# Other VectorE durations in the build-time planner of a two-layer graph kernel

## The chip, the cores and the metric

The kernel runs on one core of one Trainium2 chip. The metric is the device time of one launch in microseconds (us), and the median of the runs of the kernel before is 1470.73 us.

## What is computed

There are 16 graphs of 1024 nodes with 64 channels each, and a dense 1024x1024 adjacency per graph that is mostly zero. The mask is all ones in the given inputs.

```python
h = max(layernorm(x), 0)
x = x + matmul(adj / clip(adj.sum(2), 1), h)                       # layer 0
h = max(layernorm(x), 0)                                           # layer 1
nb = neighbours of each node in adj, without itself; m = their number
rows with m > 10 drop every ceil(m/2)-th neighbour, and the drop is made symmetric
agg = 0.25*q25 + 0.5*q50 + 0.25*q75 over the node itself and the neighbours left
x = x + (relu((h + agg) @ W1 + b1) @ W2 + b2) * mask
```

The quantiles are taken per node and per channel over a list whose length differs from node to node.

## The kernel before, in words

**Layer 0 (eight streams, lines 574 to 823).** Each graph is taken in eight blocks of 128 adjacency rows. `loads` brings a block in (SP queue), `signs` makes a 16-bit sign copy of it on ScalarE, `listing` (line 631) multiplies that by a key on VectorE (`sg<-sg,keyed`) and takes the eight largest of four segments with MAX8 (`rec<-sg`), which lists the neighbours. `transposes` and `products` make the matmul on TensorE, with evacuations on ScalarE; `channels` makes the layernorm of layer 1; `endings` (line 751) sorts the nodes of a graph by list length in a chain of small VectorE operations and scatters their rows with eight indirect DMAs per graph from the POOL queue (`srt<-row,to`).

**Layer 1 (class `Job`, line 845).** The graphs form four groups of four. `group` (line 1187) prepares a group's tables once its four graphs are through. A job then takes the nodes whose lists have one length. It gathers the neighbours' rows, one indirect DMA per 128 rows and place (`places<-tab,idx`, POOL queue), masks and weighs them on VectorE, sorts them in `passes` (line 982) with a min/max network of `tensor_tensor` operations, weighs the sorted places, and sends the sums through TensorE and ScalarE (`layers`, line 1124) to an indirect scatter into the output (`out_dram<-y`). Four long jobs at the end (`long_lists`, line 1324; tiles `lplaces`, `lother`, `l0other`) serve the few nodes with 16 to 88 neighbours. A network operation is 64 channels wide times the number of 128-row tiles in the job times the pairs that it takes at once, so most of them are 64 to 512 elements wide in each partition.

**What sets the order.** VectorE's and POOL's instructions are kept in the order in which the Python program issues them (`tc.manual_schedule`), and the program issues them in the order of a planner, which is no part of what runs on the chip. Every piece of work is a generator, a stream, that yields an engine and a function that tells from when it could run. `Plan.run` (line 335) takes, again and again, the stream with the smallest pair of planned start and rank: a start is the larger of the engine's planned clock and the time that the stream names. `Plan.note` (line 283) moves the clock of the engine forward by the planned duration of each instruction, and says that its output can be read `after` later. POOL's indirect DMAs are planned at 1.27 us, with 2.2 us to landing. Streams ask for margins: `SLACK` 2 us after an operand from another engine, `LOOSE` 7 us, `LATE` 14 us (lines 227 to 229). Jobs rank ahead of layer 0 while fewer than `AHEAD` = 16 gathers are outstanding and behind it otherwise (`later` and `soon`, lines 913 to 919). Buffers count too: there are four `places`, four `sg`, five `at`, six `y` tiles.

`passes` does not let `note` look at tiles. It keeps its own table of places and says (line 996) that a network operation's result can be used 0.15 us after VectorE's planned clock:

```python
soon = max(done.get(key, begin) for key in near)
yield "DVE", lambda: soon, self.later
...
done.update(((copy, i + shift), plan.clock["DVE"] + 0.15) for i in each)
```

`spread` (line 201) is called by `network` (line 155) once per network, ahead of the planner. It puts the operations of one network into the order in which the planner gets them: the one whose operands are ready first, the first of the list among equals.

All instructions of the planned part have line L240 in the profile, the line of the wrapper, so groups are told apart by their tiles. A slow path for graphs that don't fit the lists (`dense_path`) is behind a branch that isn't taken.

Of the kernel before, what the change touches and what calls it, by code (L numbers as in the profile page):

```python
# [125 lines left out]
def numbers(run):  # L126
    first, d1, n1, d2, n2 = run
    return [first + d2 * k2 + d1 * k1 for k2 in range(n2) for k1 in range(n1)]
# [26 lines left out]
def network(n, width, block=None):  # L155
# [16 lines left out]
    for layer in reversed(layers):  # L172
# [17 lines left out]
        for (part, _, is_max, *kind), left in sorted(kinds.items()):  # L190
# [3 lines left out]
            )  # L194
    parts = [
        spread([op for p, op in ops if p == part], width) for part in range(1 + -(-n // block))
    ]
    return parts, count, at


def spread(ops, width):

    left, order = list(ops), []
    clock, ready = 0.0, {}
    while left:
        best, reads, writes = None, set(), set()
        for k, (op, ai, aj, dist, copy, run) in enumerate(left):
            run = numbers(run)
            near = {(ai, i) for i in run} | {(aj, i + dist) for i in run}
            out = {(copy, i + (dist if op == OP.max else 0)) for i in run}  # L210
            if not (near & writes or out & (reads | writes)):
                begin = max(clock, *(ready.get(key, 0.0) for key in near))
                if best is None or begin < best[0]:
                    best = begin, k, out
            reads |= near
            writes |= out
        begin, k, out = best
        clock = begin + 0.07 + len(numbers(left[k][5])) * width * 1.04e-3
        ready.update((key, clock + 0.15) for key in out)
        order.append(left.pop(k))  # L220
    return order
# [24 lines left out]
class Plan:  # L246
# [36 lines left out]
    def note(self, engine, op, args, kwargs):  # L283
        if self.own is not None:
            self.clock[engine] = max(self.clock[engine], self.own)
        out = kwargs["out"] if "out" in kwargs else args[0]
        rest = [*args[0 if "out" in kwargs else 1:], *(v for k, v in kwargs.items() if k != "out")]
        rest = [getattr(v, "ap", v) if type(v).__name__.startswith("Indirect") else v for v in rest]
        rest = [v for v in rest if isinstance(v, bass.AP)]
        size = max(math.prod(v.shape[1:]) for v in (out, *rest[:2]))  # L290
        start = max(
            self.clock[engine],
            *(self.ready.get(v.tensor.name, 0.0) for v in rest if self.own is None),
            self.used.get(out.tensor.name, 0.0) if self.own is None else 0.0,
        )
        after = 0.15
        apart = engine == "SP" and out.tensor.name in self.parts
        if apart:
            start = max(self.clock[engine], *(self.ready[v.tensor.name] for v in rest))
        if engine == "DVE":  # L300
            half = op == "tensor_tensor" and all(v.dtype == HF for v in (out, *rest))
            time = 0.04 if op == "memset" else 0.07 + size * (0.57e-3 if half else 1.04e-3)
        elif engine == "ACT":
            pointers = sum(isinstance(kwargs.get(k), bass.AP) for k in ("bias", "scale"))
            time = 0.06 + size * 0.86e-3 + 0.11 * pointers + 0.09 * ("accum_out" in kwargs)
        elif engine == "PE":
            time = 0.1 + math.prod(out.shape[1:]) * 0.88e-3
            if op == "matmul" and rest[0].dtype == F32:
                time *= 2
        elif engine == "POOL":  # L310
            time, after = (1.27, 2.2) if op == "indirect_dma_start" else (0.15, 0.1)
            self.last = None
        else:
            start = max(start, self.clock["DMA"])
            busy = math.prod(out.shape) * 4 / 165e3

            time, after = 0.05, 2.2 + busy * (1 if 4 * out.shape[-1] >= 512 else 2)
            self.clock["DMA"] = start + busy
        self.clock[engine] = end = start + time
        if not apart:  # L320
            self.ready[out.tensor.name] = end + after
        for v in rest:
            self.used[v.tensor.name] = max(self.used.get(v.tensor.name, 0.0), end + after)
        if "accum_out" in kwargs:
            self.ready[kwargs["accum_out"].tensor.name] = end + after
        return start
# [1438 lines left out]
```

## Time and profile before

| what | value |
|---|---|
| median of 3 runs | 1470.73 us (1468.12 to 1472.69) |
| the profiled execution's own time | 1469.38 us |
| its span | 1467.6 us |
| VectorE (DVE) | 1267.8 us busy, 86%, 4263 instructions |
| GpSimd (POOL) | 939.3 us busy, 64%, 1112 instructions |
| TensorE matmul (PE) | 738.8 us busy, 50% |
| ScalarE (ACT) | 577.8 us busy, 39% |
| indirect gathers of `places` and `lplaces` | 621, from 213.94 us on, the last one ends at 1379.5 us |

A record gives an instruction's start and end. Where records of one engine lie over each other, the busy time counts the stretch once. POOL's busy time holds the records of its indirect DMAs, and a DMA that is issued right behind another starts 0.30 us after the end of that one's record, so 1.25 us pass from start to start of two gathers in a row.

### The profile page before, as it was taken

What the parts mean: (1) busy time and instruction counts of PE and PEld (TensorE: products, weight loads), DVE (VectorE), ACT (ScalarE), POOL (GpSimd) and SP (SyncE); (2) the same over time, 40 slices, a digit from 0 to 9 for tenths busy, and PEclk for the clock granted to TensorE, in tenths of its full rate; (3) what the DMA queues carried; (4) which work ended last, traced back from release to release, by engine and by line L of the source; (5) the groups of instructions that cost most, each with busy time, mean ns of one, the idle gap of its engine ahead of it and who ended that gap; (6) DMA issues with size and microseconds to landing.
All of it is one profiled execution on the core that took longest, in us unless ns stands there. A gap on an engine that the chain in (4) does not pass through costs nothing.

```text
span 1467.6 us, 14957 instructions
## 1 busy us (share of the span) xinstructions
PE 738.8 (50%) x3186; PEld 460.6 (31%) x3186; DVE 1267.8 (86%) x4263; ACT 577.8 (39%) x1747; POOL 939.3 (64%) x1112
## 2 busy tenths in 40 slices
PE   4778777228778347683585663200510101224864
PEld 2444334214445224352353332100410001123753
DVE  6878799999999895899959967588999998999895
ACT  7989879245666324783454432000100000000110
POOL 0132227777767777577876777477777787778432
PEclk9889898559989558895598676555665555555876
DMA  5446667424464224465233232321211111221000
GB/s 175 150 145 185 163 192 196 119 67 112 135 164 141 66 51 112 129 194 136 69 93 96 82 71 48 63 68 41 43 39 24 25 30 31 44 46 24 16 11 11
DMA packets 134591, 132.22 MB, mean 90 GB/s; under 512 B 100196, under 2 KB 102884, under 8 KB 134372
## 3 DMA queue, kind: packets, MB, share of 16 engines
q1 hardware_dynamic: 102972, 91.00, 21.6%
q0 software_dynamic: 31520, 40.19, 12.6%
q14 instruction: 72, 0.59, 0.1%
q8 instruction: 27, 0.44, 0.1%
HBM read 111.62 MB, written 23.61 MB: 92 GB/s over the span
## 4 chain that ended last, share of the span: by engine, by line
DVE 44%; POOL 19%; issue 11%; ACT 10%; DMA 9%; PE 5%; SPq 1%; DVEq 0%; POOLq 0%; ACTq 0%
POOL places L240 11%; DVE places L240 7%; DVE other L240 6%; DVE lplaces L240 5%; DVE rec L240 5%; DMA at<-in_adj_dram 4%; DMA places<-tab,idx 4%; POOL lplaces L240 4%; ACT sg L240 3%; PE pt L240 3%; ACT ln_sq L240 2%; DVE l0other L240 2%; DVE sg L240 2%; POOL out_dram L240 2%; PE ps_small L240 2%
## 5 line engine op out<-in xcount | busy, mean ns | idle before, releaser
L240 POOL DMA_INDIRECT places<-tab,idx x372 | 371.6, 999 | 115.5 <-issue 105.7
L240 PE MATMUL pt<-ident,prod 128*128 128x128 f32 (+1 forms) x736 | 162.5, 384 | 396.4 <-DVE prod L240 320.3
L240 PEld LDWEIGHTS pt<-ident,prod 128*128 128x128 f32 (+1 forms) x736 | 132.9, 264 | 428.1 <-issue 255.7
L240 PE MATMUL ps_small<-att,h 128*65 128x512 f32 x512 | 255.0, 645 | 14.1 <-ACT att L240 6.7
L240 POOL DMA_INDIRECT srt<-row,to x128 | 128.1, 1001 | 178.5 <-ACT row L240 156.0
L240 PE MATMUL pt<-ident,at 128*128 128x128 f32 x1024 | 167.1, 308 | 93.9 <-ACT att L240 71.7
L240 DVE MAX8 rec<-sg 128x8 f16<-128x256 f16 x512 | 180.2, 414 | 4.4
L240 PEld LDWEIGHTS pt<-ident,at 128*128 128x128 f32 x1024 | 128.0, 156 | 139.0 <-ACT att L240 95.3
L240 ACT ACTIVATE sg<-at 128x1024 f16<-128x1024 f32 x128 | 135.0, 1055 | 89.9 <-DMA at<-in_adj_dram 69.6
L240 POOL DMA_INDIRECT lplaces<-whole,lidx x125 | 132.1, 1057 | 38.3 <-issue 37.4
L240 POOL DMA_INDIRECT places<-tab,last_idx x124 | 126.2, 1018 | 37.8 <-issue 36.3
L240 ACT COPY att<-pt 128x512 f32<-128x512 f32 x256 | 141.4, 583 | 19.0 <-PE pt L240 17.6
L240 PEld LDWEIGHTS ps_small<-att,h 128*65 128x65 f32 x512 | 74.0, 151 | 148.2 <-issue 119.7
L240 ACT COPY ot<-pt 128x128 f32<-128x128 f32 (+3 forms) x56 | 22.4, 399 | 230.2 <-PE pt L240 228.1
L240 DVE TENSOR_TENSOR sg<-sg,keyed 128x1024 f16<-128x1024 f16 x128 | 87.3, 682 | 29.4 <-ACT sg L240 29.3
L240 POOL DMA_INDIRECT out_dram<-y,nodes_i x93 | 97.0, 1043 | 21.0 <-issue 13.9
L240 ACT ACTIVATE wu<-wu 128x39 f32<-128x39 f32 (+9 forms) x40 | 9.5, 237 | 255.2 <-DVE wu L240 255.2
L240 PE MATMUL ps_small<-ot,w_sb 128*128 128x128 f32 (+3 forms) x112 | 49.4, 531 | 100.4 <-DVE y L240 84.1
L240 ACT ACTIVATE hid<-ps_small,b_sb 128x128 f32<-128x128 f32 (+2 forms) x56 | 28.1, 504 | 126.3 <-PE ps_small L240 126.0
L240 DVE TENSOR_TENSOR other<-places,other 128x64 f32<-128x64 f32 (+6 forms) x204 | 69.4, 340 | 5.4
L240 DVE TENSOR_TENSOR places<-places,other 128x64 f32<-128x64 f32 (+2 forms) x208 | 62.3, 309 | 4.8
L240 DVE TENSOR_TENSOR places<-other,places 128x128 f32<-128x128 f32 (+5 forms) x160 | 54.9, 343 | 3.4
(269 smaller groups left out, 1651.3 us busy)
## 6 DMA issues: line engine op xcount, KB each, us to landing
at<-in_adj_dram SPq DMA_DIRECT2D x128, 512.0 KB
places<-tab,idx POOLq DMA_INDIRECT x372
whole<-tab SPq DMA_DIRECT2D x4, 1057.0 KB
tab<-row SPq DMA_DIRECT2D x16, 264.0 KB
xt<-in_x_dram SPq DMA_DIRECT2D x16, 256.0 KB
srt<-row,to POOLq DMA_INDIRECT x128
lplaces<-whole,lidx POOLq DMA_INDIRECT x125
places<-tab,last_idx POOLq DMA_INDIRECT x124
```

Of the source, the lines that this page charges most:

```text
L240: ins = getattr(self._engine, op)(*args, **kwargs)
```

## The change

Six numbers in the planner. In `spread` the fixed part of a network operation goes from 0.07 to 0.15 us. In `note` the fixed part of a VectorE operation goes from 0.07 to 0.12 us (0.10 where all operands are 16-bit in a `tensor_tensor`), that of a `memset` from 0.04 to 0.06 us, and the time until its output can be read from 0.15 to 0.05 us. The factors per element stay. The 0.15 in `spread`'s `ready` and in `passes` (line 996), and the 0.07 with which `passes` decides where to put a small `memset` (line 999), stay too. No instruction is added or taken away; VectorE's and POOL's can come in another order.

```diff
@@ spread @@
-        clock = begin + 0.07 + len(numbers(left[k][5])) * width * 1.04e-3
+        clock = begin + 0.15 + len(numbers(left[k][5])) * width * 1.04e-3
         ready.update((key, clock + 0.15) for key in out)
@@ Plan.note @@
         if engine == "DVE":
+            after = 0.05
             half = op == "tensor_tensor" and all(v.dtype == HF for v in (out, *rest))
-            time = 0.04 if op == "memset" else 0.07 + size * (0.57e-3 if half else 1.04e-3)
+            time = 0.06 if op == "memset" else (
+                0.1 + size * 0.57e-3 if half else 0.12 + size * 1.04e-3
+            )
```

## Prediction

> **What bounds the kernel now.** I read the page's slices first, then the waits of the two queues that the planner orders, then the timeline of VectorE for what one instruction costs its queue.
>
> ```profile
> DVE  6878799999999895899959967588999998999895
> POOL 0132227777767777577876777477777787778432
> ...
> DVE 44%; POOL 19%; issue 11%; ACT 10%; DMA 9%; PE 5%; SPq 1%; DVEq 0%; POOLq 0%; ACTq 0%
> ```
>
> In 40 slices of 36.7 us VectorE is at 9 tenths from the sixth slice on, with holes in slices 16, 21 and 24 to 26. POOL stands mostly at 7, and that is full: a gather's record is 0.94 us, and 0.30 us of issue lie between two (the longest line below: 466 such gaps, 142.0 us). From 213.94 to 1379.5 us the timeline shows 837 indirect DMAs on POOL and 12 waits above 0.5 us, 57.8 us in all. VectorE in the same stretch has 19 waits above 1 us, 82.3 us in all. The chain ends on both. The kernel is a two-queue pipeline with 5 to 7% of air, and the order of the queues decides where the air is.
>
> ```profile
> POOL places L240 <- issue: 142.0, 466, 0.3
> POOL lplaces L240 <- issue: 37.4, 122, 0.6
> POOL srt L240 <- ACT row L240: 25.0, 14, 10.2
> ...
> POOL gat_rows L240 <- DVE gfound L240: 14.8, 1, 14.8
> ```
>
> ```profile
> DVE sg L240 <- ACT sg L240: 22.1, 3, 8.7
> DVE rem L240 <- DMA places<-tab,idx: 11.4, 5, 3.6
> DVE gat_rows L240 <- DMA gat_rows<-in_adj_dram,lnodes_i: 10.9, 3, 5.6
> DVE y L240 <- PE ps_small L240: 10.8, 2, 6.0
> DVE deg L240 <- PE ps_small L240: 9.2, 1, 9.2
> ```
>
> Both are the waits between 213 and 1380 us (engine, tile, what ended the wait, us in total, times, longest). After 1214 us VectorE has only 4.8 us of such waits up to 1380 us: the end is a VectorE backlog, so what VectorE loses before it is mostly lost for good.
>
> **What an instruction costs VectorE's queue.** The timeline of one network, 64 elements wide:
>
> ```profile
> 496.76 0.23 DVE L240 TENSOR_TENSOR other<-other,places 128x64 f32<-128x64 f32 x1
> 496.90 0.22 DVE L240 TENSOR_TENSOR places<-places 128x64 f32<-128x64 f32 x1
> 497.03 0.23 DVE L240 TENSOR_TENSOR other<-places 128x64 f32<-128x64 f32 x1
> 497.29 0.23 DVE L240 TENSOR_TENSOR other<-other,places 128x64 f32<-128x64 f32 x1
> ```
>
> Each record is 0.22 us long, but 496.76, 496.90 and 497.03 lie 0.14 and 0.13 us apart: an instruction starts some 82 ns before the record in front of it ends, unless it needs that one's result; then it starts 34 ns behind its end (497.03 to 497.29). Over all network operations of that width: 139 unheld ones start 139 ns apart, 244 held ones 261 ns. So the slot is 0.07 us + 1.04 ns per element, and a result costs 122 ns more when the next instruction wants it at once. At 256 elements it is the same: 340 and 459 ns.
>
> [...]So durations "of the trace" and the time that a queue loses differ, and a planner's clock wants the latter.
>
> **The change, part by part.** It issues the same instructions; all cost is order.
>
> *The spread of a network.* It changes only where one put-between operation was too short to cover 0.15 us: 0.07 + w x 1.04e-3 is below 0.15 for w under 77, so for 64 alone, by 13 ns. Jobs of two or more tiles have no operation below 128 and keep their order exactly. 383 operations of 64 elements are concerned; on the chip one put-between slot (139 ns) covers the 122 ns, so the new rule is the truer one here. If one in ten changes between held and unheld: 38 x 0.122 = 4.7 us, either sign. I take 0, and keep 5 us each way; the cover of anything lost is VectorE's own air, and there is little.
>
> *The clock of VectorE in the planner.* I put the width of each of the 4262 records that have a successor into both formulas, and the 1778 held ones (646 of them network operations) into both delays. Old: elements 793.8 + 3965 x 0.07 + 297 memsets x 0.04 + 1778 x 0.15 = 1350.0 us. New: 793.8 + 3837 x 0.12 + 128 x 0.10 + 297 x 0.06 + 646 x 0.15 + 1132 x 0.05 = 1438.4 us. The trace, first start to last start less the waits above 0.15 us: 1333.0 us. So the old clock is 1.3% slow, the new one 7.9%. By kind: a chain of small operations is planned nearer (0.17 for a true 0.186 us; old 0.22), an unheld network operation farther (0.187 for 0.139 at width 64), and so is a MAX8 (386 for 331 ns, 512 of them).
>
> *What a slow clock does.* In the planner, VectorE comes 88.4/1333.0 = 6.6% later to everything; on the chip it comes earlier than planned to what ScalarE, TensorE and the DMAs make for it, whose durations aren't changed. An in-order queue then waits with everything behind it: behind `sg<-sg,keyed` stand the MAX8s, the chains of `endings`, the networks of running jobs, and behind those PE (`pt`), ScalarE (`wu`), POOL's scatter and the `places` tiles that POOL needs. Graphs 5 to 16 are scattered between 230 and 920 us, one each 706/12 = 59 us. If the slip builds up over a graph and its buffers tie it back: 59 x 0.066 = 3.9 us, of which `SLACK` covers 2.0, leaves 1.9 us x 12 = 23 us. Below: 0, where the buffers tie it back at each block. I take half, 11 us (my choice: the three `sg` waits show that the margin is already used up in some graphs, not in all).
>
> *POOL.* Its scatters are planned behind VectorE's results, so a slow VectorE clock puts them behind more gathers. That is worth some of the 25.0 + 14.8 us above, and makes tiles `y` and `row` come free later. I take 0; bounds -20 and +10 us. Of the first 214 us nothing is expected: VectorE has 34 us of air there, and POOL waits for ScalarE's `row`.
>
> Sum against the profiled execution: 1469.4 + 0 + 11 + 0 = 1480.4 us. Its time lies 1.3 us under the median of the runs, so 1481.7, rounded to 1482 us.
>
> **The rivals.**
>
> *Faster: fewer empty places in the plan.* A held operation follows its producer at once when the planner has nothing else ready. With the new clock VectorE is never ahead: of 346 us from 214 to 560, the formula without delays fills 273 in the old plan and 327 in the new. More streams then stand ready, and get between producer and consumer. 646 held network operations at 122 ns are 79 us; a quarter filled is 20 us, so 1451 us. For it: VectorE's backlog at the end, which takes over any gain. Against it: the chains of 15 and 10 places, with one pair at a time, have no neighbour once layer 0 has given its block.
>
> *No change.* The ranks decide in both plans since both are full; air moves, and the sum stays: 1471 us.
>
> *Clearly slower: a group's preparation comes late.* POOL waited 17.2 and 17.3 us for VectorE ahead of its first gather at 213.9 us. The same chain stands in front of each group. If for one group the gathers in hand run out before VectorE is through, POOL stands for that whole chain: 35 us, 1506 us. It decides from the point at which the earlier group's gathers end before the next one's `tab` is written; in this trace POOL waited only 5.5 us for it at 424 us and 2.8 us at 677 us.
>
> *The change doesn't do what it says.* It names the trace's durations, but 0.12 is neither a record's fixed part (0.15) nor a slot's (0.07). This is no separate time; it is why I expect no gain by truth.
>
> **Chances.** Slower by the slip 40%, clearly slower 10%, no change 12%, faster 38%. A measurement of this kernel can tell about 0.3%, 4.4 us, from no change. Slower 0.50, same 0.12, faster 0.38. The likeliest case alone has 1474 to 1494 us; with both signs likely, the range for 8 in 10 reaches from 1448 (the rival's 20 us and 3 more) to 1503 us.
>
> **What would show it.** Slip: the waits of VectorE for `sg`, `deg`, `ln_v` and `y` between 213 and 1214 us grow from 47 us to 58 or more while POOL's 57.8 us hardly move. Filling: held network operations fall from 646 below 500 and the last gather still ends near 1379 us. A late group: one wait of POOL above 15 us ahead of a `gat_rows` or `tab`. Networks of two or more tiles in another order of their own would prove the argument on width wrong. I am wrong if VectorE's waits fall.

## The result, and the profile after

The changed kernel takes 1486.75 us, the median of 4 runs (1484.63 to 1488.12), against 1469.42 us of the kernel before (4 runs, 1467.38 to 1472.69) measured with it: a ratio of 1.012 with a 95% interval of 1.0095 to 1.0145, or 17.3 us (14.0 to 21.3 on 1469.4 us). The profiled execution took 1484.63 us with a span of 1482.9 us. In several of the later measurements the kernel before itself took 1874 to 1909 us instead of 1470, for a cause that stayed unknown, so each ratio below stands only for the level that is named beside it, and as a ratio leaves out runs more than 1.5% above the fastest of their kernel, it can differ from that of the medians.

The slices of the kernel after:

```profile
DVE  6878798899988989997849985598999968999996
POOL 0132228777765877775676877576777777777512
```

Slice 33 of VectorE (1186 to 1223 us) is new: a 6 behind four 9s, where the kernel before has a 9. In the last slice VectorE has a 6 in place of a 5. Counted over all records:

| us | before | after |
|---|---|---|
| VectorE occupied (first start to last start, less its waits above 0.15 us, each less 34 ns, the median that a held instruction stands in both traces) | 1333.0 | 1333.7 |
| VectorE's waits above 0.15 us, counted so | 125.6 | 142.0 |
| held network operations (number) | 646 | 664 |
| POOL's waits above 0.5 us, 214 us to its last gather | 57.8 | 66.0 |
| end of POOL's last gather | 1379.5 | 1379.4 |
| from there to VectorE's last start | 80.2 | 97.4 |
| span | 1467.6 | 1482.9 |

So the work is the same, POOL is through at the same time, and VectorE lost 16.4 us more in waits, which then lie as unfinished work behind the last gather: VectorE's last start is 17.2 us farther behind it, of which 1.6 us are waits there and the rest is work. (The change is not quite order alone: VectorE has 4260 records in place of 4263, three small `memset` of `idle` fewer, and POOL one `memset` of `turn` more, since the program places these by the same numbers. At 59 and 121 ns each, the means of their records in the kernel after, they are no part of the 17 us.) The waits of VectorE from 213 to 1380 us in the kernel after (engine, tile, what ended the wait; us in total, times, longest):

```profile
DVE sg L240 <- ACT sg L240: 22.4, 4, 14.8
DVE rem L240 <- DMA places<-tab,idx: 13.0, 7, 7.9
DVE rem L240 <- DMA places<-tab,last_idx: 12.3, 2, 11.5
...
DVE y L240 <- PE ps_small L240: 10.3, 3, 6.1
...
DVE deg L240 <- PE ps_small L240: 8.0, 2, 5.1
```

The line for `sg` is as large as before (22.1 us), that for `deg` smaller (9.2). What is new is the third line (1.5 us before): VectorE waits for gathers of the last group. Over the whole run its waits at `rem`, the first instruction that reads gathered rows, grew from 12.9 to 25.9 us, 13.0 of the 16.4 us; one for `nodes<-recs` adds 4.1, one for `rev` 2.0. Almost all of the 12.3 us is one wait. The timelines of VectorE and of POOL around it, kernel after (start, duration, operation; in brackets the idle time ahead and what ended it):

```profile
1191.77 0.61 DVE L240 TENSOR_TENSOR lplaces<-l0other 128x448 f32<-128x448 f32 x1
1192.33 0.06 DVE L240 MEMSET idle<- 128x1 f32 x1
1203.88 0.19 DVE L240 TENSOR_TENSOR rem<-places,last_recs 128x30 f32<-128x30 f32 x1 [11.48 <-DMA places<-tab,last_idx]
```

```profile
1189.56 1.16 POOL L240 DMA_INDIRECT lplaces<-whole,lidx  x1 [0.30 <-issue]
1191.02 1.08 POOL L240 DMA_INDIRECT out_dram<-y,nodes_i  x1 [0.30 <-issue]
...
1198.73 0.98 POOL L240 DMA_INDIRECT lplaces<-whole,lidx  x1 [0.30 <-issue]
1200.01 0.96 POOL L240 DMA_INDIRECT lplaces<-whole,lidx  x1 [0.30 <-issue]
1201.28 0.94 POOL L240 DMA_INDIRECT places<-tab,last_idx  x1 [0.30 <-issue]
```

VectorE breaks off the long job's network (`lplaces`, `l0other`) at 1192 us and stands for 11.48 us at a job whose last gather (of 15; the first was issued at 990 us) POOL issues only at 1201.28, behind gathers of the long job and six scatters. The profile shows no operand that POOL waited for there: 0.30 us is the gap that it has ahead of other gathers too (143.8 us over 468 gaps ahead of gathers into `places`). Before, VectorE ran the long network through this time: of 1180 to 1203 us it was busy for 22.73 us, after for 12.06. The same job's last gather and its `rem` in the kernel before:

```profile
1211.53 0.94 POOL L240 DMA_INDIRECT places<-tab,last_idx  x1 [0.30 <-issue]
...
1214.20 0.19 DVE L240 TENSOR_TENSOR rem<-places,last_recs 128x30 f32<-128x30 f32 x1 [1.34 <-DMA places<-tab,last_idx]
```

Why the one waits 1.34 us and the other 11.48 can be read by laying the planned start of each instruction, worked out from the planner, beside its record. In both plans the `rem` stands 5.6 us behind the issue of that gather. On the chip VectorE was ready for it 1.3 us behind the issue before, and 8.9 us ahead of it after. What differs is VectorE's planned clock:

| from 1100 us on, us | before | after |
|---|---|---|
| VectorE from 1100 to 1192 us, in the plan | 89.7 | 100.0 |
| the same in the trace | 91.2 | 91.4 |
| VectorE against its plan, from 1100 us to this `rem` | 1.6 lost | 8.8 gained |
| POOL against its plan, from 1100 us to this gather | 9.6 lost | 8.7 lost |

POOL falls behind its plan alike in both. VectorE kept nearly to its plan before; after, the plan holds it for 9.4% slower than it is in this stretch of wide network operations, so it comes too early to the gathers. (One of 512 elements is planned at 0.65 us and takes 0.61 in the trace from its start to the next one's, with or without a small `memset` between; the plan adds 0.06 for each of the 72 `memset` in the stretch.) This wait is slip, against POOL.

### The profile page after: what moved, and what is told of

It is laid out like the page before. It is cut to its first block, busy times and chain, and to the rows that moved or that the text cites. A ratio compares the mean times of both kernels' runs of the same rounds, so it can differ in the third digit from the quotient of the medians.

```text
span 1482.9 us, 14955 instructions
## 1 busy us (share of the span) xinstructions
PE 747.6 (50%) x3186; PEld 466.4 (31%) x3186; DVE 1268.4 (86%) x4260; ACT 580.5 (39%) x1747; POOL 931.8 (63%) x1113
## 4 chain that ended last, share of the span: by engine, by line
DVE 44%; POOL 18%; DMA 11%; issue 10%; ACT 8%; PE 8%; SPq 1%; DVEq 0%; POOLq 0%; ACTq 0%
POOL places L240 10%; DVE places L240 7%; DVE other L240 6%; PE ps_small L240 5%; DVE lplaces L240 5%; DMA at<-in_adj_dram 4%; DVE rec L240 4%; PE pt L240 3%; POOL lplaces L240 3%; POOL out_dram L240 3%; DMA places<-tab,idx 2%; ACT sg L240 2%; DVE lother L240 2%; ACT ln_sq L240 2%; DVE lfound L240 2%
## 5 line engine op out<-in xcount | busy, mean ns | idle before, releaser
L240 PE MATMUL pt<-ident,prod 128*128 128x128 f32 (+1 forms) x736 | 158.5, 376 | 319.1 <-DVE prod L240 306.0
L240 PEld LDWEIGHTS pt<-ident,prod 128*128 128x128 f32 (+1 forms) x736 | 129.5, 258 | 350.2 <-issue 201.1
L240 PE MATMUL pt<-ident,at 128*128 128x128 f32 x1024 | 175.8, 319 | 94.6 <-ACT att L240 79.6
L240 PEld LDWEIGHTS pt<-ident,at 128*128 128x128 f32 x1024 | 134.9, 162 | 138.4 <-ACT att L240 105.9
L240 ACT COPY att<-pt 128x512 f32<-128x512 f32 x256 | 142.0, 582 | 21.7 <-PE pt L240 19.0
L240 DVE TENSOR_TENSOR sg<-sg,keyed 128x1024 f16<-128x1024 f16 x128 | 87.4, 683 | 34.4 <-ACT sg L240 34.4
L240 POOL DMA_INDIRECT out_dram<-y,nodes_i x93 | 92.8, 997 | 21.1 <-issue 11.3
L240 PE MATMUL ps_small<-ot,w_sb 128*128 128x128 f32 (+3 forms) x112 | 49.4, 532 | 110.9 <-DVE y L240 91.2
L240 POOL DMA_INDIRECT out_dram<-y,last_nodes_i x31 | 33.3, 1075 | 44.6 <-DVE y L240 38.5
L240 PEld LDWEIGHTS ps_small<-ot,w_sb 128*128 128x128 f32 (+1 forms) x112 | 21.4, 232 | 124.0 <-DVE y L240 89.3
```

The lines of the kernel that those rows point to most:

```text
L240: ins = getattr(self._engine, op)(*args, **kwargs)
```

## The experiments

Two theories stood against each other. **Slip**: a planned clock of VectorE that is slower than the chip's makes VectorE stand for operands that aren't there yet. **Chance**: any change of a planner's number, however small, draws another order from a lot that spreads by some per cent, and the change is one draw. (The first expectations take chance more narrowly: any new order is worse than the kept one.)

**The two halves.** `e1_spread_only` and its repetition have only the number in `spread`, the `e2` kernels only those in `note`:

```diff
# e1_spread_only, e1b_spread_only
-        clock = begin + 0.07 + len(numbers(left[k][5])) * width * 1.04e-3
+        clock = begin + 0.15 + len(numbers(left[k][5])) * width * 1.04e-3
# e2_note_only, e2b_note_only, e2c_note_only
+            after = 0.05
-            time = 0.04 if op == "memset" else 0.07 + size * (0.57e-3 if half else 1.04e-3)
+            time = 0.06 if op == "memset" else (
+                0.1 + size * 0.57e-3 if half else 0.12 + size * 1.04e-3
+            )
```

> Only the 0.15 in spread, the planner's clock as before. Slip theory (the loss comes from VectorE's clock in the planner being too slow): no loss, 1465 to 1475 us, held network operations between 600 and 690. Rival, the networks' own order: most of the 17 us, 1480 or more, with held operations or their cost up. Rival, order by chance (any new order of the tuned plan is worse than the kept one): 1475 to 1490 without a reason in the trace.

> Only the planner's clock (0.12, 0.10, 0.06 and 0.05 later), spread as before. Slip theory: the whole loss, 1481 to 1493 us, VectorE's waits above 135 us against 126 before, its occupied time within 3 us of 1333. Rival, the networks' own order: 1465 to 1475 us. Rival, order by chance: anything from 1465 to 1495, not the same as with both parts.

Measured: the kernel before took 1877.24 us beside them. `e1_spread_only` took 1875.34 (20 runs), 0.1% less; its ratio, 1.0065 (1.0014 to 1.0116), compares it with the 5 fastest of 26 runs of the kernel before, so no loss is shown. `e2_note_only` took 1852.67, 1.3% less (ratio 0.9799, 0.9762 to 0.9836). By these, the numbers of `note` made the kernel faster, which no theory had foreseen, at a level on which the change itself had not been measured. Repeated later:

> Once more[...]. Only the 0.15 in spread. Slip theory: no loss, within 5 us of the kernel before. Rival, the networks' own order: most of the 17 us. Rival, order by chance: 5 to 20 us slower without a reason in the trace.

> Only the planner's clock (0.12, 0.10, 0.06 and 0.05 later), spread as before, once more. Slip theory: the whole loss, 10 to 20 us slower than the kernel before, VectorE's waits above 135 us, its occupied time as before. Rival, the networks' own order: within 5 us of the kernel before. It counts if the kernel before runs near 1470 us.

> Only the planner's clock (0.12, 0.10, 0.06 and 0.05 later), spread as before, at the level of 1470 us. Slip theory: the whole loss, 1481 to 1493 us, VectorE's waits above 135 us, its occupied time within 3 us of 1333. Rival, the networks' own order: 1465 to 1475 us. Rival, order by chance: a time between 1460 and 1500 that isn't that of the changed kernel.

`e1b_spread_only` took 1871.39 beside 1880.63 us, `e2b_note_only` 1853.66 beside 1873.89, both without an interval, and `e2c_note_only` 1883.96 beside 1909.1 (0.9874, 0.9833 to 0.9916). By the medians `note` alone is 1.3, 1.1 and 1.3% faster, so its direction and size hold at this level.

**A change too small to mean anything.** 2 ns more or less in the fixed part of an operation:

```diff
# e3_jitter_up, e3b_jitter_up, e3c_jitter_up; in e4_jitter_down 0.068
-            time = 0.04 if op == "memset" else 0.07 + size * (0.57e-3 if half else 1.04e-3)
+            time = 0.04 if op == "memset" else 0.072 + size * (0.57e-3 if half else 1.04e-3)
```

> The kernel before with 0.072 in place of 0.07 in the planner's clock, a change of 2 ns per operation, 8 us in 1350 (0.6%). Slip theory: 1.9 us of slip per graph become 0.35 us, which the margin covers: 1466 to 1474 us. Rival, order by chance: 1475 to 1490 us, as for any other order.

> The kernel before with 0.068 in place of 0.07 in the planner's clock. Slip theory: 1466 to 1474 us, if anything a little faster. Rival, order by chance: 1475 to 1490 us.

> The kernel before with 0.072 in place of 0.07 in the planner's clock, once more. Slip theory: within 5 us of the kernel before. Rival, order by chance: 5 to 20 us slower, with another order as different from before as the changed kernel's. A single look; it counts if the kernel before runs near 1470 us.

> The kernel before with 0.072 in place of 0.07 in the planner's clock, now that the kernel before runs at 1470 us again. Slip theory, with the losses of the fast and the slow clock on both sides of it: a clock that is 0.6% off is as good as the kernel before's, 1466 to 1475 us. Rival, order by chance: another order, and 5 to 20 us slower.

Measured: 2 ns up gives 1.0135 (1.0089 to 1.018), then 1.011 (1.0073 to 1.0146) and 1.0131 (1.0102 to 1.0161); 2 ns down gives 0.9872 (0.9832 to 0.9912). The kernel before took 1877.24, 1907.68, 1909.1 and 1877.24 us beside them. Laid beside the kernel before, record by record in each engine's order, 3058 of VectorE's 4263 places hold another instruction with 2 ns up, and 2948 with the change; of POOL's some 1112 it is 474 and 467: 2 ns redraw the order as thoroughly as the change does. And the order so drawn is worth 1.1 to 1.35% up in three measurements, and 1.3% down in the one of the other sign. Slip had allowed 2 ns nothing, so it doesn't account for these; that any new order is worse is false too, since 2 ns down and `note` alone are faster. At this level, a difference of a per cent says nothing about a number's truth.

**The change itself at that level.**

> The changed kernel itself, once more, as a control for the runs in which the kernel before needs near 1870 us. If those runs tell the same as the first measurement, the changed kernel is 1.0 to 1.4% slower than the kernel before here too, whatever the level, and single parts can be read from their ratios. If it is not, ratios at that level are no evidence for the time at the first level.

Measured: 1881.92 us (20 runs) beside 1878.96 (23), ratio 1.0008, 0.9948 to 1.0069. Here the loss of 1.2% is not seen, so the halves above can't be added up to it either. The waits of VectorE in this execution, whole run:

```profile
DVE sg L240 <- ACT sg L240: 71.2, 18, 42.4
DVE deg L240 <- remote: 49.2, 3, 27.3
DVE y L240 <- PE ps_small L240: 43.5, 5, 13.6
DVE deg L240 <- PE ps_small L240: 36.0, 4, 25.1
```

These are longer waits, two to four times those of the first measurement for the same tiles (34.4 us for `sg`, 20.0 for `deg`, 18.0 for `y`), and "remote" means that the profile names no instruction of the core as their end. What they waited for can't be relied on: this trace has 2311 updates of VectorE's semaphore for 2972 instructions that update it, where that of the first measurement has 2971. The orders are therefore judged by different delays at the two levels, and the ratios at the upper one are no evidence for the 17.3 us.

**A clock that is far off.** Large doses in `note`, meant to stand out from the chance of a draw:

```diff
# e8_slow_clock; in e9_fast_clock 0.02
-            time = 0.04 if op == "memset" else 0.07 + size * (0.57e-3 if half else 1.04e-3)
+            time = 0.04 if op == "memset" else 0.17 + size * (0.57e-3 if half else 1.04e-3)
```

> The kernel before with 0.17 in place of 0.07 in the planner's clock alone: 3965 x 0.10 = 397 us more on 1350 us, 29% slower than the queue is. Slip theory, by the sum of the prediction: 59 x 0.29 = 17 us per graph, less the margin of 2 us, times 12, half of it: 90 us slower than the kernel before. Rival, order by chance: within 2% of it, either side, as for any other order.

> The kernel before with 0.02 in place of 0.07 in the planner's clock alone: 198 us less, 14% faster than the queue is. Slip theory: VectorE's waits shrink and POOL's grow, as its queue is then promised results too early: between 20 us faster and 15 us slower. Rival, order by chance: within 2% of the kernel before, either side.

Measured at the level of the first measurement (the kernel before 1470.13 us, 7 runs): `e8_slow_clock` 1636.41 us, ratio 1.1144 (1.1109 to 1.1178), +166.3 us; `e9_fast_clock` 1503.81 us, ratio 1.0225 (1.02 to 1.025), +33.7 us. By the prediction's way of reckoning, with 3965 operations concerned, the planned total is 1350.0 + 396.5 = 1746.5 us in the one and 1350.0 - 198.3 = 1151.7 us in the other, against 1333.0 us occupied:

| planned clock against the trace | kernel | time, us |
|---|---|---|
| 13.6% fast | e9_fast_clock | 1503.81 |
| 1.3% slow | before | 1469.42, 1470.13 |
| 7.9% slow | after | 1486.75 |
| 31.0% slow | e8_slow_clock | 1636.41 |

For the slow dose slip is right and chance is not: 11% is far outside the 1.3% of the draws above. Its 166 us are more than the half of the slip sum that I expected (90 us), and less than the whole of it (59 x 29.7% = 17.5, less 2, by 12: 186 us). For the fast dose I was wrong: I had allowed it 15 us of loss at most and expected VectorE's waits to shrink, but it lost 33.7 us and the waits grew from 125.6 to 152.9. That is 2.25%, only a little more than the 2% that chance allows for. VectorE's waits in the slow one, whole run:

```profile
DVE rem L240 <- DMA places<-tab,idx: 72.4, 17, 10.3
DVE sg L240 <- ACT sg L240: 48.4, 24, 6.6
DVE deg L240 <- PE ps_small L240: 34.5, 8, 11.0
DVE ln_v L240 <- ACT ln_sq L240: 32.9, 12, 5.7
DVE rem L240 <- DMA places<-tab,last_idx: 28.0, 5, 12.2
```

The operands named in the prediction (`sg`, `deg`, `ln_v`, `y`) grow here, from 84.6 to 145.3 us over the whole run; the gathers grow more, from 12.9 to 100.4. VectorE's waits are 162.3 us longer in all and its occupied time is 1336.3 us, so again the whole loss is waiting. POOL in its turn stands for VectorE in this kernel, while its last gather ends at 1455.6 us, 76 us later than before:

```profile
POOL out_dram L240 <- DVE y L240: 177.7, 10, 68.4
```

That was 30.8 us before: the two queues wait for each other, VectorE 100.4 us for gathers and POOL 177.7 us for `y`. How the two feed one another I did not take apart. The fast one loses in another place. Its VectorE and POOL waits, whole run:

```profile
DVE y L240 <- PE ps_small L240: 59.6, 11, 13.3
DVE ln_v L240 <- ACT ln_sq L240: 21.7, 7, 4.2
DVE sg L240 <- ACT sg L240: 17.4, 15, 3.1
```

```profile
...
POOL places L240 <- DVE rem L240: 26.7, 2, 18.7
POOL gat_rows L240 <- DVE nodes_i L240: 26.3, 3, 16.4
...
POOL tab L240 <- DVE ln_v L240: 17.4, 1, 17.4
```

Planned too fast, VectorE is late to POOL: between its first and its last gather POOL waits 131.3 us (57.8 before), the last gather ends at 1465.6 us, 86 us later than before, and VectorE's last start comes only 28.2 us after it (80.2 before). POOL has become the bound.

## Why the prediction was right, and where it wasn't

**The sign and the size** are right: 11 us forecast for the profiled execution, 15.3 measured there (1484.63 less 1469.38), 17.3 between the medians. That the loss is order, and that what VectorE loses before 1214 us is lost for good, is shown: the same occupied time, the same end of POOL's gathers, +16.4 us of waits, +15.3 us of span.

**The spread of a network, taken at 0.** The argument on width is right. Worked out from the planner, the networks of jobs with two or more tiles keep their order, and of the single-tile ones those of 9, 11 and 16 places change in 18 of 38, 6 of 43 and 6 of 63 positions, the long ones in 7 to 19. Held network operations went from 646 to 664, 18 x 0.122 = 2.2 us, within my 5; but occupied time rose by 0.7 only. Taken alone, at the upper level, it moved the median of all runs by 0.1%, which is neither a loss nor a gain. The rival that the networks' own order made the loss is not borne out there, where the change as a whole costs nothing either.

**The planned clock, 1.3% and 7.9% slow.** The totals are right and hid something: by stretches of the kernel before, the old formula gives 255.0 and the new one 272.0 for 272.6 us occupied from 920 to 1214 us. In that stretch as a whole the old numbers were 6.5% fast and the new ones true; from 214 to 560 us they are 356.5 and 380.4 for 342.8. The truth of the new ones from 920 to 1214 us is itself a sum of two errors: up to 1100 us, where the long lists are made, both clocks are about a tenth fast (a MATCH_REPLACE8 of `lkey` is planned at 0.20 us by the old formula and at 0.25 by the new, and its 40 records have 0.71 in the mean), and in the networks behind that the new one is 9.4% slow, the old one 1.6% fast. That makes the slip uneven over the run, which the step took as even, and the one wait of 11.48 us lies just where the new clock is the slow one.

**What a slow clock does: the step that failed.** It said that the waits for `sg`, `deg`, `ln_v` and `y` between 213 and 1214 us grow from 47 to 58 us or more. They fell to 42.6. The lines for `sg` and `deg` stand above (22.1 and 9.2 before, 22.4 and 8.0 after); those for `y` and `ln_v` from 213 to 1214 us, before and after:

```profile
DVE y L240 <- PE ps_small L240: 6.0, 1, 6.0
DVE ln_v L240 <- ACT ln_v L240: 5.5, 3, 2.6
DVE ln_v L240 <- ACT ln_sq L240: 4.0, 2, 2.8
```

```profile
DVE y L240 <- PE ps_small L240: 6.1, 1, 6.1
DVE ln_v L240 <- ACT ln_sq L240: 5.5, 2, 2.8
...
DVE ln_v L240 <- ACT ln_v L240: 0.6, 2, 0.3
```

What grew instead are the waits for gathers, 13.0 us: VectorE against POOL, not VectorE against ScalarE and TensorE. The slow clock did make VectorE early, at the wait of 11.48 us by 8.9 us ahead of the gather's issue, but the operands that it missed were POOL's. The prediction had put this pair under POOL, with VectorE early and POOL's scatters behind more gathers, and taken 0 for it. VectorE's waits grew in two stretches, 214 to 560 us (3.1 to 14.2 us) and 920 to 1214 us (25.7 to 37.0), and fell from 560 to 920 us (49.2 to 42.2), which isn't 12 equal parts, one for each graph.

**Why the number was near all the same.** By luck: the path that the 11 us were reckoned for cost nothing, and the half of 23 us was a choice. A straight line from before through the slow dose would give the change 6.6/29.7 x 166.3 = 37 us, the slip sum 23, the measurement 17.3, and a draw of a new order of about 1.3%, as it was seen at the upper level, some 19 us of either sign. At 31% the slow clock is the cause; at 7.9%, slip and draw fit the size of the loss alike. What the plan laid beside the trace adds is that the largest single wait, 11.48 of the 16.4 us, comes of the slow clock. The other changes of waits, up and down, were not traced so. Nor is it known whether a slow clock costs this much as a rule: another order from nearly the same numbers might have had no such wait, or a longer one. The run that would tell is several orders with 2 ns of change at the level of 1470 us, and none of the jitter kernels met that level. So what is shown is where the 17 us went, that the largest part went there because VectorE was planned too slow, and that the clocks far off in either direction cost time (166.3 us at 31.0% slow, 33.7 us at 13.6% fast); that 7.9% is worth 17 us is not shown. How `spread` and `note` share them at that level is open too.

**The rivals.** Filling is false: held network operations rose, where the rival needed fewer than 500. No change is false at the level of the first measurement, since the interval begins at 1.0095. The late group preparation showed its sign and not its size: POOL stood 12.3 us for one group's `tab`, under the 15 I had named and far from 35. The kernel after, POOL's waits from 213 to 1380 us:

```profile
POOL places L240 <- issue: 143.8, 468, 1.4
...
POOL tab L240 <- DVE y L240: 15.5, 2, 12.3
...
POOL gat_rows L240 <- DVE gfound L240: 13.5, 1, 13.5
...
POOL gat_rows L240 <- DVE deg L240: 9.3, 1, 9.3
```

As POOL's last gather still ended at 1379.4 us, these cost it nothing at the end. **That the change doesn't do what it says** holds in part: more than two queues moved. Besides VectorE and POOL, ScalarE's order differs at 1067 of 1747 places, TensorE's at 1527 of 3186 and that of the SP queue at 104 of its 295 transfers, since all their streams are drawn by the same planner.

## What to carry to other kernels

A record's duration isn't the time that a queue loses: in the kernel after, a network operation of 64 elements has a record of 0.22 us, and the next one starts 0.141 us behind its start, or 0.260 us if it needs the result. A planner wants the distance from start to start, and the extra time when the next instruction needs the result at once, both read from the timeline. Greedy planning turned a change of 2 ns into another order of the whole kernel (3058 of VectorE's 4263 places), so measure several draws before one is credited to a number's meaning, and distrust a gain or loss no larger than their spread. When an order got worse, compare the occupied time first, then the waits by what ended them, and look at the largest wait on both queues at once: the gather's place in POOL's queue explained what VectorE's queue alone could not. Then lay the plan beside the trace there. A total that comes out true can be two errors that cancel; the stretch ahead of the wait shows which queue gained on its plan and which fell behind.

## What the runs showed of the hardware

The slots of VectorE hold in the changed order too. At 64 elements an unheld network operation starts 140.7 ns after the one ahead and a held one 259.8 ns (before: 139 and 261), at 256 elements 341 and 458.5 ns (340 and 459). And one kernel on one chip took 1470.13 us at one time and 1909.1 us some minutes later. It was not profiled at the upper level, but the other orders were, and VectorE is occupied there for 1334 to 1342 us, in spans of 1858.0 to 1928.5 us, against 1333.0 of 1467.6 in the kernel before: the added time is waiting, but for 9 us at most. What lengthens these waits stayed open.
